# A four-layer graph network on one core: one transfer for the weights, small loads in the queue of loads, and some exponents and feature work on ScalarE

## The chip, the core and the metric

The kernel runs on one core of a Trainium2 chip. The core has five engines with their own instruction streams: TensorE (PE, matrix products, with weight loads that overlap them, PEld), VectorE (DVE), ScalarE (ACT), GpSimd (POOL) and SyncE (SP), which here only issues transfers. Sixteen DMA engines move data between memory and the on-chip buffer (SBUF). The metric is the device time of one launch in microseconds (us), the median of several runs.

## The reference

There are 3327 nodes with 64 features each, and one sparse matrix `adj` of 3327 x 3327 (about one entry in 200, symmetric in its pattern, values from 0.05 to 1). Four layers follow each other. Each takes `h = relu(layernorm(x))` and adds its result to `x`:

```python
# layer 0, twice, with relu after each
m = adj @ (h @ W);  gi = m @ wih.T + bih;  gh = h @ whh.T + bhh
r, z = sigmoid(i_r + h_r), sigmoid(i_z + h_z)
n = tanh(i_n + r * h_n);  h = relu((1 - z) * n + z * h)
# layer 1
support = h @ weight
mask = adj != 0;  rank = cumsum(mask, axis=1);  deg = rank[:, -1:]
k = minimum(deg, 100);  pos = rank - (deg - k)
out = (mask * where(pos > 0, 0.5 ** (k - pos), 0)) @ support + bias
# layer 2, for three pairs (W, b)
x = ((adj * adj) @ x) @ W.T + b
# layer 3, twice
x = tanh(concat([adj @ x, x]) @ W[k])
```

So there are eight products of an N x N matrix with N x 64 features, called hops 0 to 7 below: two plain, one ranked (each neighbour weighs one half to the power of the number of neighbours after it), three with squared entries, two plain.

## The kernel before, in words

**Tiles.** N is padded to 3328 = 26 blocks of 128. The host lays `adj` out transposed, so a tile is 128 sources (partitions) by some destinations. The destinations form two halves `s` of 13 blocks, and TensorE works on both halves at once, 64 output rows for each. The 13 blocks are cut into four chunks of 3, 3, 3 and 4 blocks, and the chunks into two groups: group 0 (chunks 0 and 1, tiles of 2 x 768 floats, 768 KB) and group 1 (chunks 2 and 3, 2 x 896 floats, 896 KB). A source counts as its group's own if its block lies in that group's chunks, else as foreign.

**Loads.** `adj` doesn't fit into SBUF, so its tiles are read again and again. There are 20 slots; SyncE's queue fills them in the order in which they are used, up to 28 steps ahead, as far as slots are free. A slot is free when the last user of its tile is done, and slots also serve as rooms for masks, squares and the GRU's gates.

**Order of the work.** Most hops run in pairs on one loading of the tiles (`joint`): hop 0 of group 0 alone, hops 0 and 1 of group 1, hops 1 and 2 of group 0, hops 2 and 3 of group 1, and so on. `run` builds the whole program as one list of steps (hop, chunk, tile). For each it issues loads, prepares coming tiles, expands the next two or three into operands and then emits the matmuls (L486). Whatever belongs to features is a Python generator, a task: `yield 12.0` means that the task goes on when the emitted steps sum up to 12 us of matmul by a fixed price. So a yield moves instructions in the emitted order; it is no wait on the chip. Each engine executes its own instructions strictly in that order.

**Weights and biases.** The task `more_constants` (L136) borrows a free slot, reads the 22 weight matrices of 64 x 64 into it twice, for partitions 0 to 63 and for 64 to 127 (L142, SyncE's queue), and the bias columns likewise (L143, ScalarE's queue). ScalarE's queue also reads the three bias rows, broadcast to all partitions (L144). After `yield 12.0` the copies into the block-diagonal matrices `bd` follow (L151), and a row made from a bias column by DVE (L169) and TensorE (L172, through the helper `mm`, L201).

**The ranked hop.** While hop 0 runs, DVE turns each tile into a 0/1 mask (L353) and TensorE counts neighbours per block (L420, matrix `behind`); the counts end in `totals` (`count_done`). For the ranked hop DVE makes the masks again, without row 127, and row 127 is filled from `totals` by a 3 KB transfer in GpSimd's queue (L358), 52 in all. `expand` multiplies the mask by a triangular matrix `tri` (L396 by way of L201); its result, relative to a bias and cut off at zero, holds the bits of a bfloat16 power of two. This cut, called the exponent `e`, is one instruction per half `s`: ACT's ReLU with bias (L400), or DVE's add and maximum (L398) where this holds:

```python
if s and (c == GROUPS[t.g][1] or (t.g == 0 and chunk_of(t.q % NB) in GROUPS[0])):
```

So ACT takes every first half, and the second half goes to DVE for the second chunk of either group, and for own sources of group 0. The ranked matmuls then use features split into three bfloat16 terms (`in_three`). The last row of each of the 26 source blocks has no place in its own mask; all these rows form one extra step (`SPECIAL`) with its own operand `lastw`: `mask_last` loads the 26 last rows for both halves (two transfers of SyncE's queue) and makes a mask of them, and `count_done` subtracts the counts (DVE) and cuts off (ACT), chunk by chunk.

**Features' work.** `after_1` follows hop 1 of each chunk: a GRU (`gru`), the residual, a layernorm with ReLU (`layernorm_relu`), and the split into three terms. `evacuate` copies a finished sum out of its bank, by ACT for odd chunks (L620), by DVE for even ones (L622).

Of the kernel before, what the change touches and what calls it, by code (L numbers as in the profile page):

```python
# [43 lines left out]
P = 128  # L44
# [35 lines left out]
def chunk_of(b):  # L80
    return next(c for c, (b0, b1) in enumerate(CH) if b0 <= b < b1)
# [7 lines left out]
def kernel(  # L89
# [46 lines left out]
    def more_constants():  # L136
        nc.gpsimd.memset(bd, 0.0)
        yield 5.0
        i = dead.pop()
        packed = slots[i].rearrange("p s w -> p (s w)")[:, :NW * D].rearrange("p (w f) -> p w f", f=D)  # L140
        for h in range(2):
            nc.sync.dma_start(out=packed[h * D:(h + 1) * D], in_=weights)  # L142
            nc.scalar.dma_start(out=bcol[h * D:(h + 1) * D], in_=bias_cols)  # L143
        nc.scalar.dma_start(  # L144
            out=brow[:, 0:3],
            in_=bass.AP(tensor=bias_rows.tensor, offset=bias_rows.offset, ap=[[0, P], [D, 3], [1, D]]),
        )
        yield 12.0
        for h in range(2):
            hs = slice(h * D, (h + 1) * D)  # L150
            nc.vector.tensor_copy(bd[hs, :, hs], packed[hs])  # L151
        dead.append(i)

        full = work.tile([P, P], BF16, name="t2")
        nc.gpsimd.memset(full, -TWO7)
        nc.gpsimd.affine_select(out=tri, in_=full, pattern=[[-1, P]], compare_op=ALU.is_gt, fill=0.0,
                                base=0, channel_multiplier=1)
        nc.gpsimd.affine_select(out=tri, in_=tri, pattern=[[-1, P]], compare_op=ALU.not_equal, fill=TWO7 * TWO7,
                                base=0, channel_multiplier=1)
        nc.gpsimd.memset(tri[:, P - 1:P], 0.0)  # L160
        nc.gpsimd.memset(bitsb, BITS)
        nc.gpsimd.memset(lasty, 0.0)
        wide = work.tile([P, P], F32, name="t2")
        nc.gpsimd.memset(wide, 0.0)

        for i, (bi, bh) in enumerate(((BI1, BH1), (BI2, BH2))):
            nc.vector.tensor_add(bsum[:, i], bcol[:, bi:bi + 2], bcol[:, bh:bh + 2])

        nc.vector.tensor_scalar(wide[0:D], wide[0:D], bcol[0:D, BL1:BL1 + 1], None, op0=ALU.add)  # L169
        yield 3.0  # L170
        i, ps = take()
        mm(ps[:, :D], wide, ident[:, :D])  # L172
        nc.vector.tensor_copy(brow[:, 3], ps[:, :D])
        give(i)

        for wt, ih in ((W1, IH1), (W2, IH2)):
            yield 1.0
            i, ps = take()
            mm(ps[:, :P], bd[:, wt, :], ident)
            tr = work.tile([P, P], F32, name="t2")  # L180
            nc.scalar.copy(tr, ps[:, :P])
            give(i)
            yield 1.0
            i, ps = take()
            mm(ps[:, :3 * P], tr, bd[:, ih:ih + 3, :].rearrange("p g f -> p (g f)"))
            nc.vector.tensor_copy(bd[:, ih:ih + 3, :].rearrange("p g f -> p (g f)"), ps[:, :3 * P])
            give(i)


    def blocks(c):  # L190
# [26 lines left out]
    def give(i):  # L217
        (idle_sums if i < 4 else idle_temps).append(i)
# [32 lines left out]
    def begin(c, task):  # L251
        finish(c)
        tasks[c] = [task, 0.0]
        advance(c)
# [5 lines left out]
    def later_task(us, task):  # L260
        yield us
        yield from task
# [84 lines left out]
    def make_mask(t, kind):  # L347

        t.mask = Mask(t.w)
        rows = P - 1 if kind == RANKED else P  # L350

        def piece(half):
            nc.vector.tensor_scalar(t.mask.view[:rows, half], t.view()[:rows, half], 0.0, None, op0=ALU.not_equal)  # L353
            if half == 0 and kind == RANKED:

                for ch in GROUPS[t.g]:
                    finish(("count", ch))
                nc.gpsimd.dma_start(out=t.mask.view[P - 1:P], in_=totals[t.g][t.q:t.q + D + 1:D, :])  # L358
            if half == 1:
                t.used()  # L360

        pieces.extend([(t, 0, piece), (t, 1, piece)])
# [8 lines left out]
    def expand(k, c, t):  # L371

        if k == COUNT:
            return None
        w = width(c)
        if t is SPECIAL:
            g = c // 2
            w0 = (CH[c][0] - CH[GROUPS[g][0]][0]) * P
            return lastw[g][:, w0:w0 + w].bitcast(BF16)
        if KIND[k] == PLAIN or (KIND[k] == SQUARED and t.in_place):  # L380
            return t.view(c)
        if KIND[k] == SQUARED:
            room = Mask(t.w)
            wide = room.view.rearrange("p s w -> p (s w)").bitcast(F32)[:, :2 * w].rearrange("p (s w) -> p s w", s=2)
            square(wide, t.view(c), t.q + c)
            squared[k, c, t] = room
            return wide
        wide = work.tile([P, 2, CWM], I16, name="e", bufs=3)[:, :, :w]

        mask_pieces(t=t)
        for s in range(2):
            i, ps = take()
            mm(ps[:, :w], tri, t.mask.view[:, s, t.cols(c)])  # L396
            if s and (c == GROUPS[t.g][1] or (t.g == 0 and chunk_of(t.q % NB) in GROUPS[0])):
                nc.vector.tensor_scalar(wide[:, s], ps[:, :w], BITS, 0.0, op0=ALU.add, op1=ALU.max)  # L398
            else:
                nc.scalar.activation(wide[:, s], ps[:, :w], AF.Relu, bias=bitsb)  # L400
# [26 lines left out]
    def count_done(c):  # L427
        g = c // 2
        w = width(c)
        w0 = (CH[c][0] - CH[GROUPS[g][0]][0]) * P  # L430
        i, ps = counts.pop(c)
        yield 0.8
        nc.scalar.copy(totals[g][:, w0:w0 + w], ps[:, :w])
        u = work.tile([P, CWM], F32, name="t2")[:, :w]
        nc.vector.scalar_tensor_tensor(u, ps[:, :w], -TWO7, last_masks[g][1][:, w0:w0 + w], op0=ALU.mult, op1=ALU.add)
        give(i)
        yield 0.8
        nc.scalar.activation(lastw[g][:, w0:w0 + w], u, AF.Relu, bias=bitsb)
        if c == GROUPS[g][1]:
            last_masks[g][0].free()  # L440

    last_masks = {}

    def mask_last(g):
# [5 lines left out]
        last_masks[g] = room, v  # L450
        nc.gpsimd.memset(v, 0.0)
        yield 5.0
        rows = adjT.rearrange("(q p) (s n) -> q p s n", p=P, s=2)
        for s in range(2):
            nc.sync.dma_start(out=v[s * D:s * D + NQ], in_=rows[:, P - 1, s, w0:w0 + w])
        yield 12.0
        nc.vector.tensor_scalar(v, v, 0.0, 129.0 * TWO7, op0=ALU.not_equal, op1=ALU.mult)

    def propagate(k, c, t, rhs, first, last):
        if k == COUNT:  # L460
# [153 lines left out]
            propagate(k, c, t, expanded.popleft(), n == 1, n == total[k, c])  # L614


    def evacuate(acc, c):
        m = work.tile([P, CWM], F32, name="t2")[:, :width(c)]
        if c % 2:
            nc.scalar.copy(m, acc[1][:, :width(c)])  # L620
        else:
            nc.vector.tensor_copy(m, acc[1][:, :width(c)])  # L622
        give(acc[0])
        return m
# [24 lines left out]
        give(i)  # L649
        return ft  # L650

    def layernorm_relu(h, c, scale=None, pace=1.0):
        n = 2 * blocks(c)
        v = groups(xchunk(c))
        st = work.tile([P, 4, 8], F32, name="st", bufs=4)
# [3 lines left out]
        nc.vector.tensor_tensor(xc[:, :n], v, st[:, 1, :n, None].to_broadcast([P, n, D]), ALU.subtract)  # L659
        yield 1.5 * pace  # L660
        sq = work.tile([P, 8, D], F32, name="t2")
        nc.vector.tensor_tensor(sq[:, :n], xc[:, :n], xc[:, :n], ALU.mult)  # L662
        nc.vector.tensor_reduce(st[:, 2, :n], sq[:, :n], AX.X, ALU.add)  # L663
        nc.vector.tensor_scalar(st[:, 2, :n], st[:, 2, :n], 1.0 / D, EPS, op0=ALU.mult, op1=ALU.add)  # L664
        nc.gpsimd.tensor_tensor(st[:, 3, :n], st[:, 2, :n], mhalf[:, :n], ALU.pow)  # L665
# [16 lines left out]
    def gru(acc, c, hT, ih, hh, bi, bh, cell, pace=1.0):  # L682

        w = width(c)
        m = evacuate(acc, c)
# [21 lines left out]
        nc.vector.tensor_tensor(d, d, z, ALU.mult)  # L707
        nc.vector.tensor_tensor(d, d, r, ALU.add)
        o = features(c)
        nc.vector.tensor_scalar(o, d, 0.0, None, op0=ALU.max)  # L710
        dead.append(at)
        yield 2.4 * pace
        return o
# [44 lines left out]

    def after_1(c, acc):
        pace = 1.0 if c in GROUPS[0] else 1.2  # L760
        h2T = yield from gru(acc, c, hT[c], IH2, HH2, BI2, BH2, 1, pace)
        v = transpose_to_nodes(h2T, c)
        yield 0.8 * pace
        residual(v, c)
        yk = nodes(c)
        yield from layernorm_relu(yk, c, TWO27, pace=1.2 * pace)
        add_row(c, 3)
        y[2][c] = yield from in_three(yk, c)

# [76 lines left out]
        else:  # L846
            begin(c, before_0(c))
    begin(NC, more_constants())
    begin(NC + 1, later_task(10.0, mask_last(0)))
    begin(NC + 2, later_task(60.0, mask_last(1)))  # L850
    run()
    for c in list(tasks):
        finish(c)
# [39 lines left out]
```

## Time and profile before

| | value |
|---|---|
| time, median of 3 runs | 753.79 us (753.58 to 753.99) |
| span of the profiled execution | 751.1 us |
| TensorE busy | 710.5 us (95%) |
| VectorE busy | 333.2 us (44%) |
| ScalarE busy | 233.7 us (31%) |
| GpSimd busy | 86.4 us (12%) |
| mean DMA rate | 268 GB/s |
| reads of `adj` tiles | 130 of 768 KB, 104 of 896 KB |
| exponents | 144 on ACT (mean 602 ns), 64 on DVE (mean 608 ns) |
| mask rows in GpSimd's queue | 52, issue 612 ns, landing after 3.1 us |

How to read the profile. The first part of its page gives the busy time of each engine, its share of the span and the number of instructions. The second part cuts the span into 40 equal slices of 18.8 us; a digit is the busy share of a slice in tenths, 9 being 90% or more. `PEclk` is the granted clock of TensorE in tenths. A list of waits names an engine, what it was to work on, and the engine and line that released it, then three numbers: the sum of the waits, their number and the largest. A table of stretches gives, for each stretch of time, its length, the busy time and number of instructions of PE, PEld, DVE, ACT and POOL, PE's granted clock, the share of time in which the DMA engines were busy, and the rate in GB/s. A timeline has one line per group of like instructions of an engine: start, busy time, engine, line, operation, output and inputs, shape, number, and in brackets the idle time ahead of it with its releaser.

### The profile page before, as it was taken

How to read it: one execution, taken by the hardware profiler on the slowest of the kernel's cores; microseconds unless marked ns; L12 is line 12 of the kernel's file. 1: busy time of each engine (PE TensorE's matmuls, PEld its weight loads, DVE VectorE, ACT ScalarE, POOL GpSimd, SP SyncE). 2: the span in 40 equal slices, each digit the busy share in tenths (PEclk: the TensorE clock that was granted, in tenths of full speed). 3: DMA queues.
4: the chain of work that ended last, by engine and by line, in shares of the span. 5: the costliest groups of instructions: out<-in, count | busy, mean ns of one | idle time of the engine just before them, and what ended most of it. 6: DMA issues, size and time to landing. Idle time of an engine off the chain costs nothing.

```text
span 751.1 us, 12326 instructions
## 1 busy us (share of the span) xinstructions
PE 710.5 (95%) x5072; PEld 364.4 (49%) x5072; DVE 333.2 (44%) x572; ACT 233.7 (31%) x362; POOL 86.4 (12%) x112
## 2 busy tenths in 40 slices
PE   4879999999969897999899999999999999999997
PEld 1566444443537685665534444334444454344443
DVE  6556744432894879768775113421252510000000
ACT  0001200111014675887768312840054401000000
POOL 4200000001283231212120000000010000000000
PEclk9999999999989999999999999999999999999999
DMA  8999996079575655483699929972789399907990
GB/s 317 362 371 404 405 380 234 25 287 342 188 226 184 238 193 194 140 293 114 208 312 393 332 74 393 405 292 83 264 296 365 129 405 405 395 26 244 396 391 24
DMA packets 67365, 201.54 MB, mean 268 GB/s; under 512 B 6173, under 2 KB 6917, under 8 KB 67309
## 3 DMA queue, kind: packets, MB, share of 16 engines
q1 hardware_dynamic: 64252, 199.59, 72.5%
q10 hardware_dynamic: 880, 0.96, 0.4%
q8 instruction: 40, 0.66, 0.3%
q0 software_dynamic: 2176, 0.20, 0.2%
q14 instruction: 17, 0.13, 0.0%
HBM read 199.68 MB, written 0.85 MB: 267 GB/s over the span
## 4 chain that ended last, share of the span: by engine, by line
PE 49%; DVE 3%; POOL 1%; issue 0%; ACT 0%; DVEq 0%; ACTq 0%; POOLq 0%
PE sum L486 45%; PE temp L201 4%; POOL st L665 1%; DVE adj L332 0%; DVE e L398 0%; DVE st L657 0%; DVE xs L673 0%; DVE y L669 0%; DVE st L663 0%; DVE t L662 0%; DVE t L659 0%; DVE st L658 0%; DVE xs L826 0%; DVE st L664 0%; ACT y L823 0%
## 5 line engine op out<-in xcount | busy, mean ns | idle before, releaser
L486 PE MATMUL sum<-adj,y 128*64 128x384 f32 (+1 forms) x2912 | 538.4, 515 | 15.6 <-DMA adj<-in_adjT 13.6
L486 PEld LDWEIGHTS sum<-adj,y 128*64 128x64 f32 x2912 | 220.1, 138 | 269.3 <-issue 230.2
L353 DVE TENSOR_SCALAR adj<-adj 128x768 bf16<-128x768 f32 (+3 forms) x208 | 114.7, 604 | 26.8 <-PE temp L420 26.8
L330 ACT ACTIVATE adj<-adj 128x768 f32<-128x768 f32 (+1 forms) x138 | 112.9, 886 | 40.0 <-PE sum L486 23.1
L622 DVE COPY t<-sum 128x384 f32<-128x384 f32 x16 | 8.9, 556 | 193.0 <-PE sum L486 193.0
L332 DVE TENSOR_TENSOR adj<-adj 128x768 f32<-128x768 f32 (+1 forms) x70 | 68.9, 1020 | 55.5 <-DMA adj<-in_adjT 36.8
L400 ACT ACTIVATE e<-temp,bitsb 128x384 int16<-128x384 f32 (+1 forms) x144 | 79.6, 602 | 38.9 <-PE temp L201 23.1
L486 PE MATMUL sum<-e,adj 128*64 128x384 bf16 (+1 forms) x624 | 76.0, 341 | 8.5 <-DVE e L398 6.9
L201 PE MATMUL temp<-adj,tri 128*64 128x384 bf16 (+1 forms) x416 | 63.2, 343 | 6.1 <-DVE e L398 3.9
L665 POOL TENSOR_TENSOR st<-st,mhalf 128x6 f32<-128x6 f32 (+1 forms) x16 | 26.9, 1683 | 318.6 <-DVE st L664 315.3
L486 PEld LDWEIGHTS <-adj 128*64 128x64 bf16 x624 | 44.4, 110 | 24.7 <-issue 12.7
L398 DVE TENSOR_SCALAR e<-temp 128x384 int16<-128x384 f32 (+1 forms) x64 | 38.8, 608 | 32.8 <-PE temp L201 23.5
L358 POOL DMA_DIRECT2D adj<-totals x52 | 31.7, 612 | 123.8 <-DVE adj L706 83.7
L201 PEld LDWEIGHTS <-tri 128*64 128x64 bf16 x416 | 33.2, 111 | 24.6 <-issue 15.9
L693 ACT ACTIVATE adj<-temp,bsum 128x384 f32<-128x384 f32 (+1 forms) x16 | 9.7, 608 | 106.5 <-PE temp L201 106.5
L620 ACT COPY t<-sum 128x384 f32<-128x384 f32 (+1 forms) x16 | 8.5, 533 | 90.9 <-PE sum L486 90.9
L648 ACT COPY hT<-temp 128x384 f32<-128x384 f32 (+1 forms) x12 | 6.1, 506 | 78.7 <-PE temp L201 78.7
L420 PE MATMUL temp<-adj,behind 128*64 128x384 bf16 x208 | 29.2, 343 | 0.9 <-DVE adj L353 0.9
L201 PE MATMUL temp<-bd,t 128*64 128x128 f32 (+1 forms) x320 | 26.5, 279 | 1.3 <-DVE t L622 0.9
L420 PEld LDWEIGHTS <-behind 128*64 128x64 bf16 x208 | 15.5, 111 | 19.4 <-issue 16.3
L201 PEld LDWEIGHTS temp<-bd,t 128*64 128x64 f32 x320 | 19.8, 137 | 8.6 <-DVE t L622 2.6
L201 PE MATMUL temp<-t,bd 128*64 128x384 f32 (+1 forms) x96 | 21.5, 517 | 0.1
(72 smaller groups left out, 263.9 us busy)
## 6 DMA issues: line engine op xcount, KB each, us to landing
adj<-in_adjT SPq DMA_DIRECT2D x130, 768.0 KB, 8.2
adj<-in_adjT SPq DMA_DIRECT2D x104, 896.0 KB, 10.4
adj<-in_weights SPq DMA_DIRECT2D x2, 352.0 KB
xs<-in_x SPq DMA_DIRECT2D x1, 640.0 KB
out<-xs ACTq DMA_DIRECT2D x3, 192.0 KB, 1.9
adj<-totals POOLq DMA_DIRECT2D x26, 3.0 KB, 3.1
adj<-totals POOLq DMA_DIRECT2D x26, 3.5 KB, 3.1
out<-xs ACTq DMA_DIRECT2D x1, 256.0 KB, 5.9
```

The source lines that it names most:

```text
L201: nc.tensor.matmul(out[hs], lhsT[:, hs], rhs, start=start, stop=stop)
L330: nc.scalar.activation(sq, v, AF.Square)
L332: nc.vector.tensor_tensor(sq, v, v, ALU.mult)
L353: nc.vector.tensor_scalar(t.mask.view[:rows, half], t.view()[:rows, half], 0.0, None, op0=ALU.not_equal)
L358: nc.gpsimd.dma_start(out=t.mask.view[P - 1:P], in_=totals[t.g][t.q:t.q + D + 1:D, :])
L398: nc.vector.tensor_scalar(wide[:, s], ps[:, :w], BITS, 0.0, op0=ALU.add, op1=ALU.max)
L400: nc.scalar.activation(wide[:, s], ps[:, :w], AF.Relu, bias=bitsb)
L420: nc.tensor.matmul(counts[c][1][s * D:(s + 1) * D, :w], behind[:, NQ - 1 - t.q:NQ - 1 - t.q + D], t.mask.view[:, s, t.cols(c)], start=firs ...
L486: nc.tensor.matmul(acc[h * D:(h + 1) * D, :w], yq[h], rhs[h], start=first and n == 0, stop=last and n == len(terms) - 1)
L622: nc.vector.tensor_copy(m, acc[1][:, :width(c)])
L665: nc.gpsimd.tensor_tensor(st[:, 3, :n], st[:, 2, :n], mhalf[:, :n], ALU.pow)
L693: nc.scalar.activation(gate, ps[:, :w], AF.Sigmoid, bias=bsum[:, cell, g:g + 1])
```

## The change

It has five parts. The weights come in one transfer, whose source pattern repeats the 64 rows twice (a stride of 0) and whose destination is all 128 partitions. The small loads leave ScalarE's queue, where they stood at the head of the kernel, for SyncE's: the bias columns behind the weights, the bias rows after two more yields. The mask rows leave GpSimd's queue for SyncE's, and the extra step's operand is made later: `last_sources` starts after 70 and 230 us instead of 10 and 60, in one piece per group, and `count_done` only copies the counts. Group 0's exponents of chunk 1 with foreign sources (14 of its second halves) go from DVE to ACT. And in `after_1`, the copy of a finished sum, the layernorm's squares and the GRU's last ReLU go from DVE to ACT (`busy=True`). The aim is to take waits from the front of TensorE's stream: transfers at half rate and small packets ahead of tiles, and a VectorE that is late with exponents.

```diff
@@ more_constants
+        nc.sync.dma_start(out=packed, in_=bass.AP(tensor=weights.tensor, offset=weights.offset,
+                                                  ap=[[0, 2], [NW * D, D], [1, NW * D]]))
         for h in range(2):
-            nc.sync.dma_start(out=packed[h * D:(h + 1) * D], in_=weights)
-            nc.scalar.dma_start(out=bcol[h * D:(h + 1) * D], in_=bias_cols)
-        nc.scalar.dma_start(
-            out=brow[:, 0:3],
-            in_=bass.AP(tensor=bias_rows.tensor, offset=bias_rows.offset, ap=[[0, P], [D, 3], [1, D]]),
-        )
-        yield 12.0
+            nc.sync.dma_start(out=bcol[h * D:(h + 1) * D], in_=bias_cols)
+        yield 20.0
...
+        yield 20.0
+        nc.sync.dma_start(
+            out=brow[:, 0:3],
+            in_=bass.AP(tensor=bias_rows.tensor, offset=bias_rows.offset, ap=[[0, P], [D, 3], [1, D]]),
+        )
@@ make_mask
-                nc.gpsimd.dma_start(out=t.mask.view[P - 1:P], in_=totals[t.g][t.q:t.q + D + 1:D, :])
+                nc.sync.dma_start(out=t.mask.view[P - 1:P], in_=totals[t.g][t.q:t.q + D + 1:D, :])
@@ expand
         if t is SPECIAL:
...
+            finish(NC + 1 + g)
...
-            if s and (c == GROUPS[t.g][1] or (t.g == 0 and chunk_of(t.q % NB) in GROUPS[0])):
+            own = chunk_of(t.q % NB) in GROUPS[t.g]
+            if s and (own if t.g == 0 else c == GROUPS[t.g][1]):
                 nc.vector.tensor_scalar(wide[:, s], ps[:, :w], BITS, 0.0, op0=ALU.add, op1=ALU.max)
@@ count_done
         nc.scalar.copy(totals[g][:, w0:w0 + w], ps[:, :w])
-        u = work.tile([P, CWM], F32, name="t2")[:, :w]
-        nc.vector.scalar_tensor_tensor(u, ps[:, :w], -TWO7, last_masks[g][1][:, w0:w0 + w], op0=ALU.mult, op1=ALU.add)
         give(i)
-        yield 0.8
-        nc.scalar.activation(lastw[g][:, w0:w0 + w], u, AF.Relu, bias=bitsb)
...
@@ mask_last, now last_sources
         nc.vector.tensor_scalar(v, v, 0.0, 129.0 * TWO7, op0=ALU.not_equal, op1=ALU.mult)
+        for c in GROUPS[g]:
+            finish(("count", c))
+        yield 1.0
+        nc.vector.scalar_tensor_tensor(v, totals[g], -TWO7, v, op0=ALU.mult, op1=ALU.add)
+        yield 1.5
+        nc.scalar.activation(lastw[g], v, AF.Relu, bias=bitsb)
+        room.free()
@@ evacuate, with busy=False as default
-        if c % 2:
+        if c % 2 or busy:
             nc.scalar.copy(m, acc[1][:, :width(c)])
@@ layernorm_relu, with busy=False as default
-        nc.vector.tensor_tensor(sq[:, :n], xc[:, :n], xc[:, :n], ALU.mult)
+        if busy:
+            nc.scalar.activation(sq[:, :n], xc[:, :n], AF.Square)
+        else:
+            nc.vector.tensor_tensor(sq[:, :n], xc[:, :n], xc[:, :n], ALU.mult)
@@ gru, with busy=False as default
-        nc.vector.tensor_scalar(o, d, 0.0, None, op0=ALU.max)
+        if busy:
+            nc.scalar.activation(o, d, AF.Relu)
+        else:
+            nc.vector.tensor_scalar(o, d, 0.0, None, op0=ALU.max)
@@ after_1
-        h2T = yield from gru(acc, c, hT[c], IH2, HH2, BI2, BH2, 1, pace)
+        h2T = yield from gru(acc, c, hT[c], IH2, HH2, BI2, BH2, 1, pace, busy=True)
...
-        yield from layernorm_relu(yk, c, TWO27, pace=1.2 * pace)
+        yield from layernorm_relu(yk, c, TWO27, 1.2 * pace, busy=True)
@@ the start of the tasks
-    begin(NC + 1, later_task(10.0, mask_last(0)))
-    begin(NC + 2, later_task(60.0, mask_last(1)))
+    begin(NC + 1, later_task(70.0, last_sources(0)))
+    begin(NC + 2, later_task(230.0, last_sources(1)))
```

More of the change, by code (lines that the diff above doesn't have):

```diff
@@ L433, in count_done, with last_sources @@
         nc.scalar.copy(totals[g][:, w0:w0 + w], ps[:, :w])
-        u = work.tile([P, CWM], F32, name="t2")[:, :w]
-        nc.vector.scalar_tensor_tensor(u, ps[:, :w], -TWO7, last_masks[g][1][:, w0:w0 + w], op0=ALU.mult, op1=ALU.add)
         give(i)
-        yield 0.8
-        nc.scalar.activation(lastw[g][:, w0:w0 + w], u, AF.Relu, bias=bitsb)
[L439 to L444, printed above, removed]
+    def last_sources(g):
         w = sum(width(c) for c in GROUPS[g])
@@ L449, in mask_last @@
         v = room.view.rearrange("p s w -> p (s w)").bitcast(F32)
-        last_masks[g] = room, v
         nc.gpsimd.memset(v, 0.0)
-        yield 5.0
+        yield 4.0
         rows = adjT.rearrange("(q p) (s n) -> q p s n", p=P, s=2)
@@ L614, in run, with evacuate @@
             propagate(k, c, t, expanded.popleft(), n == 1, n == total[k, c])
-    def evacuate(acc, c):
+    def evacuate(acc, c, busy=False):
         m = work.tile([P, CWM], F32, name="t2")[:, :width(c)]
-        if c % 2:
+        if c % 2 or busy:
             nc.scalar.copy(m, acc[1][:, :width(c)])
@@ L650, in transpose_to_features, with layernorm_relu @@
         return ft
-    def layernorm_relu(h, c, scale=None, pace=1.0):
+    def layernorm_relu(h, c, scale=None, pace=1.0, busy=False):
         n = 2 * blocks(c)
@@ L680, in add_row, with gru @@
                                 brow[:, i:i + 1, :].to_broadcast([P, n, D]), ALU.add)
-    def gru(acc, c, hT, ih, hh, bi, bh, cell, pace=1.0):
+    def gru(acc, c, hT, ih, hh, bi, bh, cell, pace=1.0, busy=False):
         w = width(c)
-        m = evacuate(acc, c)
+        m = evacuate(acc, c, busy)
         yield 0.8 * pace
```

## Prediction

> **What bounds the kernel now.** I read the page first. Matmuls fill 710.5 of 751.1 us, and in the 40 slices TensorE (PE) is full from slice 26 on. So time can only change where PE is not full: about 41 us, nearly all before 375 us.
>
> ```profile
> PE 710.5 (95%) x5072; PEld 364.4 (49%) x5072; DVE 333.2 (44%) x572; ACT 233.7 (31%) x362; POOL 86.4 (12%) x112
> PE   4879999999969897999899999999999999999997
> ```
>
> Next, PE's waits. The largest are for tiles of adj, for VectorE's (DVE) exponents `e`, and one for L169, the row built from the bias columns.
>
> ```profile
> PE sum L486 <- DMA adj<-in_adjT: 13.6, 8, 9.6
> PE sum L486 <- DVE e L398: 6.9, 5, 4.2
> PE temp L201 <- DVE t L169: 3.1, 1, 3.1
> PE sum L486 <- ACT e L400: 1.5, 1, 1.5
> ```
>
> Then the stretches, us by us. The last two columns are DMA share and GB/s. Around the weights the 16 DMA engines are all busy at half their rate; elsewhere up to 120 us they move about 405 GB/s. Until 66 us loads set the pace: PE works 1.62 us per tile there, a 786 KB tile takes 786/405 = 1.95 us, and PE's last wait for a tile (the 26th) ends at 66.11.
>
> ```profile
> 33.20:40.20 7.00, 4.80 (x40) 2.08 (x36) 0.00 (x0) 0.48 (x1) 0.00 (x0) 1.00 1.03 264
> 40.20:43.00 2.80, 0.00 (x0) 0.00 (x0) 2.25 (x6) 0.00 (x0) 0.00 (x0) 1.00 1.02 393
> 43.00:46.70 3.70, 3.61 (x23) 2.71 (x25) 3.70 (x9) 0.00 (x0) 0.00 (x0) 0.54 1.03 400
> 46.70:66.00 19.30, 18.76 (x149) 15.49 (x145) 11.35 (x24) 2.40 (x4) 0.00 (x0) 1.00 1.03 386
> 66.11 0.87 PE L486 MATMUL sum<-adj,y 128*64 128x384 f32 x4 [0.65 <-DMA adj<-in_adjT]
> ```
>
> Last, the timeline where group 0's ranked hop begins. PE waits 1.52 us for ScalarE (ACT) and 4.24 us for DVE, whose exponent stands behind eight mask pieces; then it runs at half clock until 227.7.
>
> ```profile
> 219.42 0.32 PE L486 MATMUL sum<-e,adj 128*64 128x384 bf16 x1 [1.52 <-ACT e L400]
> 220.59 3.83 DVE L353 TENSOR_SCALAR adj<-adj 127x768 bf16<-127x768 f32 x8
> 224.34 0.54 DVE L398 TENSOR_SCALAR e<-temp 128x384 int16<-128x384 f32 x1
> 224.93 1.12 PE L486 MATMUL sum<-e,adj 128*64 128x384 bf16 x5 [4.24 <-DVE e L398]
> ```
>
> **What the skill says.** (1) Trainium skill, "DMA: Bandwidth & Descriptors", section "Why a DMA increments its semaphore by 16 and not by 1": a transfer runs on the largest number k of engines, at most 16, that divides the outermost sizes of both its access patterns; on the hardware queues these are the lowest-numbered engines, and each posts one completion. The trace agrees where it can be counted: queue q1 has 64252 packets. Its 234 tile loads are 128 x 2 rows each, x has 256, the weights 128, the four last-row loads 26 each: 60392. The other 3860 are completions: 242 transfers x 16 would be 3872, and 12 fewer is what four transfers of 26 rows on 13 engines give.
>
> ```profile
> q1 hardware_dynamic: 64252, 199.59, 72.5%
> ```
>
> (2) "SBUF — State Buffer", section "Door 1: The DMA port swizzle": 64 partitions reach only half of the ports. The 264 GB/s above agrees; single microseconds from 34 to 38 stand at 192 to 215. (3) "TensorE: Matmul & The Clock Gate", section "What's actually happening": about 3.4 us idle halves the clock, about 3.4 us of work restores it. The 0.54 after the gap of 40 to 43 us agrees.
>
> **The change part by part.**
>
> *Weights in one transfer.* The built program reads them with outermost sizes 2, 64, 1408 and writes 128 partitions. By (1), k is 2: engines 0 and 1 carry 64 rows of 5632 B each, 360 KB, where before 16 shared 720 KB. One engine moves 405/16 = 25.3 GB/s, so 360/25.3 = 14.2 us at best. At worst those two run at half rate, as the weights did before, while the others are busy. The built order lets eight transfers be in flight, so the others get five more tiles (9.75 us) before the queue waits for the weights: 4.9 us more, 19.1. I take 16.6. Every tile uses all 16 engines, so every tile behind the weights stands behind them on two rings: this is on the path.
>
> *Small loads.* At the head, the 96 KB of bias rows go (row broadcast to 128 partitions): rates of 323, 150, 174 and 370 GB/s at 5 to 9 us miss (1620 - 1017)/405 = 1.5 us. They return at about 60 us in the queue, after tile 26, where PE has 10 us of lead (tile 27 is wanted at 78 us): nothing. The two 78 KB last-row loads of group 0 also move behind tile 26. The weights started at 33.4 us, so now at 31.9. Tile 26 lands at 31.9 + 16.6 + 12 x 1.95 + 1.2 for completion (estimate from the 2.4 us of the first, 192 KB load) = 73.1. PE's own pace gives the same: tile 15 at 51.7, then the 20.0 us that PE takes from there before (44.26 to 65.46, less 1.2 of half clock), plus 1.7 of half clock after this longer gap: 73.4. Before it was 66.1: **+7.0**, from +4.6 (14.2) to +9.5 (19.1). The wait for L169 (3.1 us) and its cold clock vanish in the longer wait: they bring nothing, since tiles set the end of this stage.
>
> *Longer yield (12 to 20).* It moves the uses of the weights behind tile 19, which lands after the weights. Nothing.
>
> *Mask rows to the load queue.* 52 issues of 612 ns leave GpSimd, which waits for others most of the time: nothing gained directly. SyncE now waits for a mask buffer's last reader, and loads queue behind that. A row took 3.1 us to land; behind loads I bound it between 2.4 (first load) and 5.6 (median load, 200 to 400 us). In the built order group 0's rows stand over 100 matmuls ahead of their use: hidden. Group 1's stand 13 to 37 ahead, twice directly ahead: 0 to 3 us, less the 1.1 us that the weight load at 340 us now waits for such a row. I take +0.3.
>
> *Group 0's exponents.* Fourteen (chunk 1, foreign sources) go from DVE to ACT. The 4.24 us wait goes. So does most of the 1.52: DVE, full from 190 to 225 us, loses about 1.7 us ahead of the cast that ACT stood behind (two squares 0.55 + 0.69, one ReLU 0.43). And so does the cold clock (0.5 + 0.5 + 0.28 = 1.3 us): 7.0 together. I take back 0.9, since four exponents of 0.51 us now follow each other on ACT, and 1.0, since tiles of the plain hop, loaded when DVE's pieces free their slots, come only about 2 us earlier while PE comes 6 earlier: **-5.1** (-6.5 to -3.5).
>
> Then 233 to 269 us, group 0's remaining foreign ranked tiles beside both GRUs:
>
> ```profile
> 233.00:269.00 36.00, 33.47 (x324) 23.80 (x322) 25.08 (x52) 24.45 (x48) 8.39 (x11) 1.00 0.68 230
> ```
>
> ACT does 48 pieces in 24.45 us, 0.51 each. Twelve exponents, two squares and two ReLUs more are 16 x 0.51 = 8.2: 32.6 of 36 us. But in the 7.8 us of GRU matmuls ACT has work for only some 4.6, so beside the other 28.2 us of PE stand 28.0 us of ACT in strict order, with waits for the GRU's vector chain (3 x 0.56 us): ACT becomes the bound, **+2.0** (0 to +5).
>
> *Features' work.* The squares, ReLUs and copies of chunks 2 and 3 fall where ACT is nearly idle (178 to 215 us); for chunks 0 and 1 they are in the sum above.
>
> *Last sources later.* One 896-wide product on DVE and one ReLU on ACT, about 1 us each, move from idle to busy times near 340 us, in the 0.3 above.
>
> Sum: +7.0 - 5.1 + 2.0 + 0.3 = +4.2, from 753.8 to **758.0**.
>
> **The rivals.** (a) The weights do spread over 16 engines and 128 partitions: they cost 1.8 us instead of 1.8 + 7 x (405 - 264)/405 = 4.2, and with the 1.5 and 1.1 for small and row loads the start gains about 4.8: 753.8 - 4.8 - 5.1 + 2.0 + 0.3 = 746.2, faster. For it: 128 partitions avoid the half rate. Against: the outermost 2, and the thirteen engines counted above. (b) Two engines, but at their full 14.2 us and the ranked hop's whole 6.5 us with ACT keeping up: 753.8 + 4.6 - 6.5 + 0.3 = 752.2. For it: ACT's sum still fits into 36 us. (c) Two engines at half rate, ACT bound and a smaller gain: 753.8 + 9.5 - 3.5 + 4 = 763.8. For it: busy ports. Against: the others soon run dry.
>
> **How the numbers follow.** Forecast 0.62, (a) 0.13, (b) 0.12, (c) 0.13. The range goes from 750 to 764: it leaves out (a) and the upper tail of (c). Slower by over 0.2% (above 755.3) are nearly all of the forecast and (c): 0.74; within it 0.08, mostly from (b); faster 0.18, from (a) and the rest of (b).
>
> **What would show it.** Right: a stretch of several us between 35 and 50 with near 2/16 of 405, some 50 GB/s, one PE wait of over 10 us for a tile, PE past tile 26 at 71 to 75 us, no wait on DVE exponents near 215, and PE waiting on ACT exponents from there to 270. Wrong: full DMA rate through 30 to 60 us with PE past tile 26 by 63 us would mean (a); rows of `totals` as PE's releaser after 290 us would mean that the load queue costs more than I allow.

## The result, and the profile after

The changed kernel takes 761.22 us (759.77 to 761.98, 4 runs), the kernel before 753.89 in the same series: a ratio of 1.0093, 95% interval 1.0072 to 1.0113. So it is 7.3 us slower, where 4.2 were forecast, inside the range of 750 to 764. The profiled execution is the fastest of the four (759.77).

The page of the changed kernel: engines and TensorE's slices.

```profile
PE 708.6 (93%) x5072; PEld 355.1 (47%) x5072; DVE 319.4 (42%) x546; ACT 243.5 (32%) x384; POOL 59.4 (8%) x60
...
PE   5819999999999898989999999999999999999997
```

TensorE does the same 5072 matmuls and is busy for 1.9 us less (710.5 before); its idle time grew by 8.9 us, and the span by 7.0. One slice, the third (38 to 57 us), is down to 1, and the dip of before in the twelfth (6, 207 to 225 us) is gone. The waits, of the changed kernel and then one line of the kernel before:

```profile
PE sum L488 <- DMA adj<-in_adjT: 19.1, 3, 17.4
PE sum L488 <- DVE y L674: 9.2, 2, 8.1
PE temp L203 <- DMA adj<-totals: 3.6, 1, 3.6
PE sum L488 <- DVE e L402: 2.6, 4, 0.9
```

```profile
PE temp L201 <- DMA adj<-totals: 0.2, 1, 0.2
```

The line of 9.2 is mostly the wait for the first matmul, 8.10 us instead of 9.57; before it was put down to a tile. New are one wait of 17.4 us for a tile and one of 3.6 us for a mask row (0.2 before); the waits of ranked matmuls for VectorE's exponents fell from 6.9 to 2.6.

To see where time comes and goes I use the lag: the start of the n-th matmul in a kernel less the start of the n-th matmul in the kernel before, from the two traces. Here it is at four matmuls, named by their time in the kernel before:

| kernel | 85 us (480th) | 249 us (1480th) | 268 us (1680th) | 353 us (2440th) | median time |
|---|---|---|---|---|---|
| changed | +8.7 | +1.8 | +4.0 | +6.9 | 761.2 |
| e1 weights in 128 rows | -7.4 | -14.8 | -12.5 | -8.7 | 744.9 |
| e2 two loads | -4.1 | -11.8 | -9.5 | -5.7 | 746.7 |
| e3 before, one transfer | +12.7 | +13.4 | +13.4 | +13.2 | 765.8 |
| e4 old rule | +9.1 | +6.5 | +6.9 | +10.8 | 763.9 |
| e5 rows by GpSimd | +8.7 | +2.6 | +4.9 | +5.8 | 758.1 |
| e6 not busy | +8.1 | +1.7 | +1.6 | +5.9 | 758.9 |
| e7 128 rows, rows by GpSimd | -7.5 | -12.1 | -9.8 | -9.1 | 743.0 |
| e8 old rule, not busy | +9.3 | +7.8 | +7.8 | +11.8 | 764.5 |
| e9 three parts | -7.2 | -11.1 | -11.2 | -11.0 | 743.0 |
| e10 two parts | -7.3 | -11.4 | -11.5 | -6.7 | 745.4 |
| e11 yield 12 | +11.0 | +4.1 | +6.3 | +11.5 | 762.1 |
| e12 no engine moves | +9.1 | +10.3 | +10.3 | +10.6 | 763.0 |

Read along the first row, the changed kernel loses 8.7 us at the start, wins 6.9 by 249 us, loses 2.3 by 268 and 2.8 by 353; after that no row moves by more than 0.6. The experiments take these four apart. In them, "before" is run again on the same chip (753.3 to 753.8 us). Each row is one execution. Executions of one kernel differ by 0.3 us (e3) to 4.0 us (e11), the longer ones with a lower mean clock (e11: 760.43 us at 0.988, 764.45 at 0.980), so a difference of about 1 us between two rows counts only where several pairs repeat it.

Stretches of the changed kernel, with the columns of the table shown before:

```profile
37.00:54.00 17.00, 0.00 (x0) 0.00 (x0) 0.64 (x2) 0.00 (x0) 0.00 (x0) 0.59 0.72 190
54.00:70.00 16.00, 15.94 (x120) 8.74 (x122) 9.48 (x21) 0.85 (x2) 0.00 (x0) 0.90 1.01 391
233.00:269.00 36.00, 31.83 (x292) 19.99 (x293) 17.51 (x35) 26.93 (x56) 9.19 (x10) 1.00 0.63 211
```

For 17 us TensorE does nothing, while the DMA engines move 190 GB/s instead of 400; its clock is half for most of that time, and still for a part of the next stretch (0.90).

### The profile page after: what moved, and what is told of

Its sections match the earlier page's. It is cut to its first block, busy times and chain, and to the rows that moved or that the text cites. A ratio compares the mean times of both kernels' runs of the same rounds, so it can differ in the third digit from the quotient of the medians.

```text
span 758.1 us, 12271 instructions
## 1 busy us (share of the span) xinstructions
PE 708.6 (93%) x5072; PEld 355.1 (47%) x5072; DVE 319.4 (42%) x546; ACT 243.5 (32%) x384; POOL 59.4 (8%) x60
## 4 chain that ended last, share of the span: by engine, by line
PE 49%; DVE 3%; POOL 1%; issue 0%; ACT 0%; DVEq 0%; ACTq 0%; POOLq 0%
PE sum L488 45%; PE temp L203 4%; POOL st L670 1%; DVE adj L334 0%; DVE e L402 0%; DVE st L659 0%; DVE xs L678 0%; DVE y L674 0%; DVE st L668 0%; DVE t L667 0%; DVE t L661 0%; DVE st L660 0%; DVE xs L834 0%; DVE adj L355 0%; DVE st L669 0%
## 5 line engine op out<-in xcount | busy, mean ns | idle before, releaser
L488 PE MATMUL sum<-adj,y 128*64 128x384 f32 (+1 forms) x2912 | 536.7, 515 | 29.2 <-DMA adj<-in_adjT 19.1
L488 PEld LDWEIGHTS sum<-adj,y 128*64 128x64 f32 x2912 | 214.3, 138 | 287.5 <-issue 238.7
L355 DVE TENSOR_SCALAR adj<-adj 128x768 bf16<-128x768 f32 (+3 forms) x208 | 114.8, 602 | 50.9 <-PE temp L424 50.5
L332 ACT ACTIVATE adj<-adj 128x768 f32<-128x768 f32 (+1 forms) x138 | 113.0, 887 | 39.8 <-DMA adj<-in_adjT 18.9
L404 ACT ACTIVATE e<-temp,bitsb 128x384 int16<-128x384 f32 (+1 forms) x158 | 86.2, 612 | 32.1 <-PE temp L203 16.1
L402 DVE TENSOR_SCALAR e<-temp 128x512 int16<-128x512 f32 (+1 forms) x50 | 31.2, 623 | 24.7 <-ACT e L404 14.4
L424 PE MATMUL temp<-adj,behind 128*64 128x384 bf16 x208 | 27.4, 339 | 1.7 <-DVE adj L355 1.7
L424 PEld LDWEIGHTS <-behind 128*64 128x64 bf16 x208 | 13.7, 110 | 21.0 <-issue 18.8
L704 DVE SCALAR_TENSOR_TENSOR adj<-temp,bcol,adj 128x384 f32<-128x384 f32 (+1 forms) x8 | 5.2, 651 | 40.5 <-PE temp L203 40.5
```

The source lines that it names most:

```text
L332: nc.scalar.activation(sq, v, AF.Square)
L424: nc.tensor.matmul(counts[c][1][s * D:(s + 1) * D, :w], behind[:, NQ - 1 - t.q:NQ - 1 - t.q + D], t.mask.view[:, s, t.cols(c)], start=firs ...
L488: nc.tensor.matmul(acc[h * D:(h + 1) * D, :w], yq[h], rhs[h], start=first and n == 0, stop=last and n == len(terms) - 1)
```

## Experiments at the start: who carries the weights

**e1**, the changed kernel with the weights laid out twice by the host, so that one plain transfer fills 128 partitions:

```diff
-        nc.sync.dma_start(out=packed, in_=bass.AP(tensor=weights.tensor, offset=weights.offset,
-                                                  ap=[[0, 2], [NW * D, D], [1, NW * D]]))
+        nc.sync.dma_start(out=packed, in_=weights)
...
-        "in_weights": np.ascontiguousarray(np.stack(mats, axis=1)),
+        "in_weights": np.ascontiguousarray(np.concatenate([np.stack(mats, axis=1)] * 2)),
```

> The changed kernel with one edit: the host lays the weights out twice, as 128 rows, and the one transfer reads them without the repeat of stride 0. Theory (the repeat has an outermost size of 2, so two DMA engines carry everything): now 16 engines carry it in about 2 us. The 17.4 us wait of TensorE near 54 us is gone, the lead over the kernel before at matmul 280 goes from +10.4 us to between -4 and -2, and the time falls from 761.2 to about 750 us. Rival (one large transfer into 128 partitions is slow by its size or its rows of 5632 B, or the small loads behind it are): the wait stays, 760 to 762 us. Second rival (the 6.9 us that the changed kernel wins near 215 to 225 us are won only because TensorE comes late there): the start is won but the wait near 215 us comes back, 755 to 758 us.

Measured: 744.87 us (ratio to before 0.9879, 0.9864 to 0.9894), 5 us below the 750 expected: at matmul 280 it is 6.5 us ahead of the kernel before, where 2 to 4 were expected. e2 shows what I had missed. The same stretch of e1:

```profile
37.00:54.00 17.00, 16.00 (x130) 8.11 (x132) 10.54 (x23) 1.14 (x4) 0.00 (x0) 1.00 1.03 400
```

The wait is gone, and with it 16.3 us of the whole. The direct evidence that the number of engines is the cause is in one line of each page, the load queue's packets, of the changed kernel and then of e1:

```profile
q1 hardware_dynamic: 64734, 199.87, 71.8%
```

```profile
q1 hardware_dynamic: 64748, 199.87, 72.7%
```

The same transfers and bytes, and the weights' 128 rows of 5632 B in both; e1 has 14 packets more. By the count of completions in the prediction, a transfer on 16 engines posts 16 and one on two posts two, which makes 14. The packets themselves show the rest: in the changed kernel the 128 rows start from 32.0 to 50.9 us, mostly 5 to 10 in each us, with a mean of 295 ns; in e1 they start within 3.2 us, with a mean of 220 ns. Two engines with 64 rows of 295 ns each are 18.9 us. And from 39.9 to 41.0 us, where nothing else starts, the rows start in pairs every 0.21 us and take 215 to 219 ns each: two at a time.

**e2**, the weights in two transfers of 64 partitions again, all else as changed:

```diff
+        for h in range(2):
+            nc.sync.dma_start(out=packed[h * D:(h + 1) * D], in_=weights)
```

> The changed kernel with the weights in two transfers of 64 partitions, as before; the small loads stay in the queue of loads. Theory (two engines are the cause): the wait near 54 us shrinks to at most 3 us; the weights go at about 264 GB/s again and cost 2.4 us more than at full rate, so 751 to 753 us. Rival (the small loads behind the weights, or the longer yield, make the wait): 759 us or more. Second rival (the later gain comes only from lateness): 755 to 758 us.

Measured: 746.70 us (0.9885 to 0.9934), below everything expected. The wait shrank to 2.69 us at 41.17 us. e2 too reads the same 64 rows of memory twice, so the double reading isn't what made the one transfer slow. Lag at 85 us: -4.1, against -7.4 with 128 rows. So half rate costs 3.3 us (I had 2.4), and everything else at the start, the small loads and the longer yield, is worth 4.1 us, not the 1.5 of the head alone: the kernel before waited 3.1 us for the row of L169, and here that wait is absent.

**e3**, the kernel before with the one transfer and nothing else:

```diff
+        nc.sync.dma_start(out=packed, in_=bass.AP(tensor=weights.tensor, offset=weights.offset,
+                                                  ap=[[0, 2], [NW * D, D], [1, NW * D]]))
         for h in range(2):
-            nc.sync.dma_start(out=packed[h * D:(h + 1) * D], in_=weights)
             nc.scalar.dma_start(out=bcol[h * D:(h + 1) * D], in_=bias_cols)
```

> The kernel before with one edit: the weights in one transfer with the repeat of stride 0. Theory, two engines carry it for about 19 us: a wait of TensorE for a tile of over 12 us before 60 us, and +9 us at matmul 480. If VectorE's lateness near 215 us is a matter of its own work, all of it reaches the end: 762 to 764 us. If a late TensorE finds VectorE ready there, up to 7 us are given back: 756 to 758 us.

Measured: 765.84 us (1.0143 to 1.0173), about 2 us above what I expected. Two lines of its timeline:

```profile
56.04 0.48 PE L202 MATMUL temp<-ident,t 128*64 128x64 f32 x4 [18.18 <-DVE t L170]
...
237.61 1.12 PE L487 MATMUL sum<-e,adj 128*64 128x384 bf16 x5 [4.24 <-DVE e L399]
```

The first: with the short yield it is the row from the bias columns that TensorE waits for, and it comes 2 us later than the tile in the changed kernel (54.06). The second rules out a rival that came up with the result, that the gain near 220 us is only a late TensorE finding VectorE ready: 13 us late, it still waits the same 4.24.

**e11**, the changed kernel with the short yield again:

```diff
             nc.sync.dma_start(out=bcol[h * D:(h + 1) * D], in_=bias_cols)
-        yield 20.0
+        yield 12.0
```

> The changed kernel with the yield behind the weights at 12 us instead of 20. The prediction put the longer yield at nothing, since the tiles behind the weights set the end of this stage: within 0.5 us of 761.2. Rival (TensorE then waits for the row made from the bias columns, which comes later than the tile by copies, a sum and a matmul, as in the kernel before with one transfer, where that wait ended 2 us later than here): 762.5 to 764 us.

Measured: 762.05 us (760.43 to 764.45). In the trace TensorE waits for the row (17.49 us, until 54.52), and the lag at 85 us is 2.3 more than in the changed kernel; but this execution was the slowest of its four (764.45), and the two medians differ by 0.8 with runs that overlap. That the order of the waits changes is shown; that the yield is worth time here is not.

## Experiments from 190 to 270 us: exponents, features and GpSimd

**e4** has the old rule for exponents, **e6** the features' work on VectorE, **e8** both, **e12** both and the mask rows in GpSimd's queue. The edits for the rule, the features' work and the rows:

```diff
-            if s and (own if t.g == 0 else c == GROUPS[t.g][1]):
+            if s and (c == GROUPS[t.g][1] or (t.g == 0 and own)):
```

```diff
-        h2T = yield from gru(acc, c, hT[c], IH2, HH2, BI2, BH2, 1, pace, busy=True)
+        h2T = yield from gru(acc, c, hT[c], IH2, HH2, BI2, BH2, 1, pace)
...
-        yield from layernorm_relu(yk, c, TWO27, 1.2 * pace, busy=True)
+        yield from layernorm_relu(yk, c, TWO27, 1.2 * pace)
```

```diff
-                nc.sync.dma_start(out=t.mask.view[P - 1:P], in_=totals[t.g][t.q:t.q + D + 1:D, :])
+                nc.gpsimd.dma_start(out=t.mask.view[P - 1:P], in_=totals[t.g][t.q:t.q + D + 1:D, :])
```

> The changed kernel with the old rule for exponents: the 14 second halves of chunk 1 with foreign sources are on VectorE again. Theory (the rule wins the 6.9 us near 215 to 225 us and costs about 2 us as ScalarE's load up to 270 us): 764 to 767 us, with waits for VectorE's exponents near 225 us back. Rival (the gain is from the features' work that left VectorE, or from TensorE's late start): within 1 us of 761.2, or 759 us if ScalarE's load goes for nothing.

> The changed kernel with the features' work of hop 1 on VectorE again (copies, squares, last ReLU), the new rule for exponents kept. Under the old rule the changed kernel still won 3.7 of its 6.9 us near 215 to 225 us. Theory (these come from the features' work, which stood on a full VectorE ahead of masks and exponents): 764 to 766 us, less up to 1 us from ScalarE's lighter load to 270 us. Rival (they come from mask rows and last sources leaving GpSimd and VectorE): within 1 us of 761.2.

> The changed kernel with the old rule for exponents and the features' work on VectorE again; the loads and rows stay as changed. Theory (the rule and the features' work together make the whole 6.9 us near 215 to 225 us, and their load on ScalarE costs 1.5 to 2.2 us to 270 us): 761.2 + 6.9 - 2 = 766 us, with the waits of 1.5 and 4.2 us back. Rival (half of the gain comes from elsewhere): 762 to 764 us.

> The changed kernel with the old rule, the features' work on VectorE and the mask rows in GpSimd's queue: only the weights, the small loads and the last sources are changed. Without the rule and the features' work 2.3 us of the 6.9 near 215 to 225 us were still won. If mask rows leaving GpSimd made these: the wait of 1.5 us for an exponent of ScalarE ahead of that of 4.2 us is back, the lag stays at +8.7 to +9.2 us across it, and the rows' loss near 342 us is gone, so 763 to 764 us. If they come from the last sources: the 1.5 us wait stays away and 761.5 to 762.5 us.

Measured: e4 763.88 us (1.0119 to 1.0150), e6 758.89 (1.0053 to 1.0105), e8 764.52 (1.0139 to 1.0170), e12 762.95 (1.0109 to 1.0145). e4 came within 0.2 us of its theory and e12 of the one with the mask rows. For e6 my theory fell: without the features' work on ScalarE I expected 764 to 766 us, and it got faster, by more than the rival's 1 us. e8 lies between what the two theories gave. Lag won from 85 to 249 us, by the table; waits and half clock are read from the traces:

- e12, none of the three moves: 1.2 lost. Both waits, 1.51 for ScalarE and 4.24 for VectorE, are there; so they don't go by the later last sources, which e12 has. The 1.2 are clock: after the second wait TensorE works 5.1 us at half clock, 2.6 in the kernel before.
- e8, mask rows out of GpSimd: 1.4 won, so this move alone is 2.7. The wait of 1.5 is gone, that of 4.24 stays. Of the 2.7, 1.6 are waits and 0.8 are clock (3.4 us at half clock).
- e6, also the new rule: 6.3 won, so the rule is 4.9. The wait of 4.24 is gone, and the half clock after it (1.7 us); a wait of 1.55 for a tile comes instead.
- the changed kernel, also the features' work: 6.9 won, 0.6 for this. It keeps a wait of 1.24 for a tile:

```profile
233.91 2.16 PE L488 MATMUL sum<-adj,y 128*64 128x384 f32 x12 [1.24 <-DMA adj<-in_adjT]
```

The shares hold for this order of the moves. With the rule and the features' work already there, the rows' move is worth only 0.8 (e5 to the changed kernel). And it is not the only thing that ends the wait of 1.5: e7 and e9 (below) both have the rows in GpSimd's queue, and the features' work on ScalarE in e7 ends it too. First e9, then e7:

```profile
212.25 1.26 PE L487 MATMUL sum<-e,adj 128*64 128x384 bf16 x7 [1.52 <-ACT e L403]
```

```profile
212.00 0.65 PE L487 MATMUL sum<-e,adj 128*64 128x384 bf16 x5 [0.15 <-ACT e L403]
```

With the old rule the features' work does more (e4 wins 2.6, e8 1.4): it shortens the wait for VectorE, without ending it. In e4:

```profile
230.86 0.65 PE L488 MATMUL sum<-e,adj 128*64 128x384 bf16 x5 [3.01 <-DVE e L402]
```

Why should 3 KB transfers in GpSimd's queue matter to TensorE? The timelines of GpSimd and VectorE in e12, rows issued by GpSimd:

```profile
210.70 1.66 POOL L360 DMA_DIRECT2D adj<-totals  x3
212.38 1.01 POOL L684 TENSOR_TENSOR xs<-xs,brow 128x384 f32<-128x384 f32 x1
...
222.04 1.47 POOL L684 TENSOR_TENSOR xs<-xs,brow 128x512 f32<-128x512 f32 x1
...
212.49 1.47 DVE L661 TENSOR_TENSOR t<-xs,st 128x512 f32<-128x512 f32 x1
...
222.32 1.61 DVE L739 TENSOR_TENSOR adj<-y,adj 128x384 bf16<-128x384 f32 x1
```

and the same instructions in e8, rows issued by SyncE:

```profile
210.86 1.10 POOL L684 TENSOR_TENSOR xs<-xs,brow 128x384 f32<-128x384 f32 x1
...
219.36 1.53 POOL L684 TENSOR_TENSOR xs<-xs,brow 128x512 f32<-128x512 f32 x1
...
212.66 0.69 DVE L661 TENSOR_TENSOR t<-xs,st 128x512 f32<-128x512 f32 x1
...
221.70 0.55 DVE L739 TENSOR_TENSOR adj<-y,adj 128x384 bf16<-128x384 f32 x1
```

GpSimd's `add_row` (L684) follows the layernorm's power, by 3.2 and 3.9 us in e12, where row issues stand between, by 1.5 and 1.9 in e8. So it falls, 1.7 and 2.0 us later, onto two products of VectorE with two inputs each. Where they overlap, VectorE's take 1.47 and 1.61 us; where not, 0.69 and 0.55: 1.84 us, on an engine that is full there and has the cast and the exponents behind it. The same two long products stand in the trace of before (1.47 at 203.40, 1.61 at 213.23), in e3, e5, e7 and e9, all with rows by GpSimd, and in none of the eight traces with rows by SyncE. The row issues themselves don't do it: in e12 a product of 128x512 at 229.06 lies wholly beside row issues and takes 0.68. The Trainium skill, "SBUF — State Buffer", section "Who interferes with whom", says it: a VectorE instruction with two SBUF inputs contends with a GpSimd instruction that reads SBUF, for the second input comes through a shared read interface. These traces agree, with the numbers above. The 1.84 us fit the 1.6 us of waits that went from e12 to e8.

**The loss from 249 to 268 us** is 2.3 in each kernel that has both the new rule and the features' work on ScalarE (changed, e1, e2, e5, e7, e11), -0.1 with the rule alone (e6, e9, e10), 0.4 with the features' work alone (e4) and 0.0 with neither (e8, e12, e3). Compared with e6, which has one of the two, it is two waits of TensorE, 1.11 and 1.13 us. The changed kernel:

```profile
253.16 0.52 ACT L716 ACTIVATE hT<-adj 128x384 f32<-128x384 f32 x1 [0.87 <-DVE adj L713]
...
253.59 2.92 ACT L404 ACTIVATE e<-temp,bitsb 128x384 int16<-128x384 f32 x6
...
254.20 0.35 PE L203 MATMUL temp<-adj,tri 128*64 128x384 bf16 x2 [1.11 <-ACT e L404]
...
256.77 1.05 ACT L404 ACTIVATE e<-temp,bitsb 128x384 int16<-128x384 f32 x2 [0.26 <-PE temp L203]
...
257.71 0.52 ACT L665 ACTIVATE t<-t 128x384 f32<-128x384 f32 x1
...
258.27 0.55 DVE L668 TENSOR_REDUCE st<-t 128x6 f32<-128x384 f32 x1 [3.29 <-ACT t L665]
...
258.93 0.55 DVE L678 TENSOR_TENSOR xs<-xs,temp 128x384 f32<-128x384 f32 x1
...
259.53 0.35 PE L203 MATMUL temp<-adj,tri 128*64 128x384 bf16 x2 [1.13 <-DVE xs L678]
```

Follow it downwards. The GRU's last ReLU (L716) stands ahead of six exponents in ScalarE's order, and ScalarE waits 0.87 us for the GRU's chain on VectorE before it; TensorE waits 1.11 us for the first of these exponents to clear a `temp` bank. Then the layernorm's square (L665) stands behind eight exponents in ScalarE's order. VectorE waits 3.29 us for it with the sum over it (L668), and behind that sum stands the residual of the next chunk (L678), which reads a `temp` bank. TensorE needs this bank, and waits 1.13 us. With ReLU and square on VectorE (e6) there is no wait above 0.6 us between 235 and 285 us, although ScalarE is as busy in this stretch, 27.08 us against 26.93:

```profile
233.00:269.00 36.00, 33.75 (x314) 21.39 (x316) 20.84 (x42) 27.08 (x56) 9.79 (x13) 1.00 0.67 233
```

In time, e6 is 2.3 us below the changed kernel, but their intervals against before overlap, so this rests on the traces; how much of it is the ReLU and how much the square was not tried apart.

## Experiments on the mask rows, and all together

**e5** is the changed kernel with the rows in GpSimd's queue.

> The changed kernel with the 52 mask rows in GpSimd's queue again. Theory (the row issued at 333.45 us moves only at 341.25 because it stands behind loads in the load queue's rings, and TensorE's lag grows by 3.8 to 5.2 us there): the wait of 3.6 us for a row near 342 us is gone, and 756 to 758 us instead of 761.2. Rival (another wait, for VectorE's exponents or for tiles, stands right behind it): 760 to 762 us.

Measured: 758.05 us (1.0049 to 1.0079), just above the 756 to 758 of the theory. The intervals of e5 and of the changed kernel against before overlap slightly, but the four pairs that differ in the rows' queue alone agree: 1.6 us less (e8 to e12), 1.9 (e1 to e7), 2.4 (e10 to e9) and 3.2 (changed to e5). The two lines of SyncE and the one of TensorE that show the loss in the changed kernel:

```profile
327.22 5.89 SPq L297 DMA_DIRECT2D adj<-in_adjT  x4
333.45 0.53 SPq L360 DMA_DIRECT2D adj<-totals  x1
...
342.25 0.52 PE L203 MATMUL temp<-adj,tri 128*64 128x384 bf16 x4 [3.61 <-DMA adj<-totals]
```

Four tiles are issued from 327.22 on, then the row at 333.45. Its two packets of 1792 B start at 341.25 and 341.50 and take 80 ns each; from 334 us until then the engines move 391 to 412 GB/s, of tiles. So a row that needs 0.1 us of two DMA engines has landed 8.1 us after its issue, behind the tiles issued ahead of it. In e5, where a row lands after 4.0 us in the median of one group and 2.4 in the other:

```profile
346.58 0.52 PE L203 MATMUL temp<-adj,tri 128*64 128x384 bf16 x4 [1.26 <-DMA adj<-totals]
```

From 268 to 353 us, kernels with rows in the load queue lose 2.8 us (changed) to 5.2 (e11), those with rows by GpSimd -0.3 (e3) to 0.9 (e5). At this wait alone it is 3.8 in the changed kernel and 5.2 in e1 and e8, where the clock is half for 3.4 us after it, which it isn't in the changed kernel's trace. Rows in the load queue also win 0.8 back near 300 us: a wait for an exponent of VectorE is 0.88 there (changed, e1, e8) instead of 1.70 (before, e7, e9).

**e7** joins the edits of e1 and e5, **e10** those of e1 and e6, and **e9** those of all three.

> The changed kernel with the weights laid out in 128 rows and the mask rows in GpSimd's queue. If the two losses add up: 744.9 less 3.8 to 5.2 us, so 739.5 to 741.5 us. If the row's wait only hides another: 744 to 745 us.

> The changed kernel with two edits: weights laid out in 128 rows, the features' work of hop 1 on VectorE; the mask rows stay in the queue of loads. Additive: 744.9 less 2.3 = 742.6 us, with the wait of 3.4 us for a row near 325 us still there.

> The changed kernel with three edits: weights laid out in 128 rows, mask rows in GpSimd's queue, the features' work of hop 1 on VectorE. If the parts add up: 743.0 less the 2.3 us of the features' work = 740.7 us. If the tile waits near 220 us take it back: 742 to 743.5 us.

Measured: e7 742.98 us (0.9845 to 0.9879), e10 745.37 (0.9867 to 0.9911), e9 742.99 (0.9841 to 0.9881). The parts don't add up: e7 is 1.9 us below e1 where 3.4 to 5.4 were expected; e10 isn't below e1, nor e9 below e7. By the table, e10 has 3.5 us less than e1 at 249 us and wins 2.4 of them back by 268. In e10 TensorE waits 2.12 us for a tile at 219.41, in e1 0.71; with the early start, tiles are what ends last there. After its wait e10 runs at half clock for 3.4 us, 1.7 us more, which e1 doesn't. What makes the tiles later without `busy=True` stays open. In e9 it is not tiles, as the rival had it, that take the gain back: the tile wait is 0.53 us (2.50 in e7), but the wait of 1.52 for ScalarE is back, with 3.4 us of half clock. Of all that ran, e7 and e9 are the fastest, 10.3 and 10.4 us below the kernel before; they can't be told apart.

## Why the prediction was right, and where its terms were off

*Weights in one transfer: right in mechanism, +9.4 instead of +7.0 at tile 26.* (TensorE reaches that tile at 75.5 us, 66.1 before; by 85 us the lag is 8.7.) Two engines carried it, as read from the outermost size and the counted completions. The term that was mis-sized is the duration: 19.0 us, at the upper bound of 19.1, where I took 16.6: a row takes 215 ns alone, about what "at best" has, and up to 453 beside tiles. The 2.4 us more are seen where PE resumes, at 54.06 instead of the 51.7 reckoned for the 15th tile. The sign I named, some 50 GB/s for several us, came only in single us (43 to 65 GB/s at 39, 40, 44 and 52 us): the other engines' tiles came in bursts between, 190 GB/s in the mean. Rival (a), the weights on 16 engines at 746.2, is what e1 built: 744.9. That it comes so near is luck: its parts are -7.4, -7.4, +2.3 and +3.8 by the table, where it had -4.8 (its own items add up to 5.0), -5.1, +2.0 and +0.3.

*Longer yield and small loads: "they bring nothing" holds only behind the long wait.* The head gave 1.47 us (1.5 said). Without the long wait, e2 shows 4.1 us for all of this together.

*Mask rows: the step that failed.* "I bound it between 2.4 and 5.6" was too short at its upper end: I took the landing of a median load, but a row issued after four tiles waits for all of them, 8.1 us. I took +0.3 for this stage and it was +2.8 (3.8 at the wait, 0.8 won back near 300 us). The sentence that would show it was named: rows of `totals` as PE's releaser after 290 us. "Nothing gained directly" by freeing GpSimd failed as well, in the other direction: the overlap shown above is worth 1.6 us of waits from e12 to e8. In the changed kernel, beside the other moves, it is 0.8 by 249 us, so it offset only a part of that error.

*Group 0's exponents: -6.9 instead of -5.1*, past my upper bound of 6.5. The 4.24 us wait went by the rule (e8 to e6), as said. The 1.52 goes with squares and a ReLU leaving VectorE, as I had it (e9 to e7), but also with the mask rows alone (e12 to e8), which I hadn't seen; the change does both. Of what I took back, the later tiles came (a wait of 1.24 us, 1.0 said), but the 0.9 for exponents that follow each other on ScalarE didn't: no wait for one stands before 249 us.

*ScalarE to 270 us: +2.3 against +2.0, in part by another mechanism.* I summed ScalarE's pieces beside TensorE's and found it just full. e6, with the same ScalarE load, loses nothing, so the sum is not the cause. The waits for the GRU's vector chain that I named are half of it (the 1.11 us). The other half (1.13) is a handover that I didn't name: VectorE behind ScalarE's square, and TensorE behind VectorE. The sign "PE waiting on ACT exponents from there to 270" shows in that one wait of 1.11 only.

The terms as measured: 8.7 - 6.9 + 2.3 + 2.8 = 6.9, against 7.0 of the spans. The errors of the first two, +1.7 and -1.8, cancel each other; that the sum misses by little more than the rows' term is in part luck.

## What to carry to other kernels

Look at the outermost sizes of a transfer's two patterns before merging transfers: a repeat of 2 there put 720 KB on two of sixteen engines, and all that uses all sixteen then waited for those two. The small transfer in a queue of large ones landed after everything issued ahead of it; count the bytes in flight, not the median landing. And when a piece of a chain moves to another engine, ask what stands ahead of it there and what stands behind its consumer: the sum of busy time doesn't tell.

## What the runs showed of the hardware that was not expected

VectorE's products with two inputs took 2.1 to 2.9 times as long (0.69 to 1.47 us, 0.55 to 1.61) while GpSimd read SBUF for an addition, and a few 3 KB transfers in GpSimd's queue were enough to shift that addition onto them. A row of the weights, 5632 B, took 220 ns in the mean when 16 engines shared the rows (e1), 295 when two engines carried them beside tiles (changed), and 399 when they went to 64 partitions at a time (e2).

And it took less idle time than the 3.4 us cited in the prediction to halve TensorE's clock, but not every time: after the 2.12 us of e10 it was half, after 2.50 us at the same place in e7 it stayed full. Where it was half, it was so for 3.41 us or a multiple (6.83, 17.07, 20.48), unless the trace ended first. So a wait of about the same length can cost 1.7 us more in one trace than in another: the row's wait of 3.6 in the changed kernel, that of 3.4 in e1.
